# Graph network kernel: another order for the first loads, the ends of the layers, the branch and the tail

## The chip, the core and the metric

The kernel is one program on one core of a Trainium2 chip. The core has five engines with a queue of instructions each: PE (TensorE: matmuls; its weight loads are shown apart, as PEld), DVE (VectorE), ACT (ScalarE), POOL (GpSimd) and SP (SyncE, which only issues DMAs here). An engine takes its queue in order; semaphores make it wait for others. The metric is the device time of one execution in microseconds (us); smaller is better.

## The reference

Inputs are `x` (12,500 nodes x 256 features), 200,000 edges `src` -> `dst` sorted by `dst`, and weights. First come three layers that mix a node with the mean of its neighbours, then a norm, then one step of an attention over the same edges, and a second norm:

```python
def sage(x, Ws, Wn, b):
    agg  = segment_sum(x[src], dst)                # sum of the rows of the neighbours
    mean = agg / max(degree, 1)
    return x @ Ws + mean @ Wn + b

h = relu(sage(x, W0..)); h = relu(sage(h, W1..)); h = sage(h, W2..)
Z = layernorm(x + h)

ZU = einsum('nd,kdr->knr', Z, U)                   # 4 heads of 16
zs, zd = ZU[:, src], ZU[:, dst]
alpha = segment_softmax((zs * zd).sum(-1) / 4, dst)
agg = segment_sum(alpha * zs, dst)                 # per head
Zh  = .5 * Z + .5 * sum_k softmax(head_w)[k] * agg_k @ U_k.T
r   = Zh - (Zh @ Dmat.T) @ Dmat
out = layernorm(Z + relu(Zh + .5 * (r @ Dmat) - .05))
```

## The kernel before

**Groups of edges.** The sorted edges are cut into NG = 112 groups of GE = 1792: 128 partitions times GT = 14 columns (the last group has LT = 9 columns). For a group, `gather` (line 121) fetches the rows of its sources: 14 indirect DMAs on POOL, each for 128 edges, with the indices of one column of the list `srcI`. `onehot` (line 459, op in line 462) compares the edges' destinations with the 128 nodes that the group may hold; matmuls of that one-hot matrix with the gathered rows sum them by node into the PSUM tile `pA` (lines 866 and 874). A node whose edges straddle two groups is completed by `carry` (line 465), which adds the sum of the group before, shifted. `srcI` and `dstI` are lists that hold `src` and `dst` in this order of partition, group and column: pieces of 14 indices, 56 bytes, 128 x 111 of them in each.

**Preparation (lines 186 to 326).** The two lists are loaded on SP and ACT, then `dst` once more as `dall` in rows of 1600, from which DVE makes the start of each group (`rel`, `delta`, `starts`) and a flag that chooses between a fast and a general program. The weights of the attention are folded into two matrices `gz` and `gu` by PE and DVE. Meanwhile POOL gathers the rows of the first G0 = 3 groups into three buffers `xg` with a small list `src0` of their own. The same three buffers then rotate through all three layers.

**Layers (`fast_sage`).** Only a part of the nodes goes by gathers: 90 groups in layer 0, and 76 in layers 1 and 2. The last 20 or 32 blocks of 128 nodes are swept densely (`px`, line 755) with tables of edge counts, which are formed in layer 0 (`form`, with small gathers `el`). A group is a generator, `group(g)`, which yields at fixed points: gathers, one-hot and sums of the first half (7 columns); sums of the second half and carry; counts inverted, `mean` (line 908) and, in layer 0, a copy `agg` for the carry; transposes (`turned`, line 356); the four products with the two weight matrices (`sage_products`, line 349), `hn` and its store on SP as `hs_d`, which the next layer gathers from (`h_d`). The list `turns` in the loop says in which order the generators are advanced: `late` is group g-1, `now` is g, `far` is g-3 and exists only in layer 2, whose norm and projection follow. Between turns, units of the sweeps and the table work are put in. `chained` forces PE to take the groups' matmuls in the order of these turns. After the last group come one or two further rounds for the groups left over. In the last groups of layer 1, which the count table of layer 0 does not cover, 14 small matmuls (line 887) count the edges with `pT` as their target. Layer 2's last step writes `z_d`, its transpose `zt_d` and the projection `zu_d`.

**Branch and attention (`fast_attention`, line 969 on).** After layer 2 a maximum is compared with a bound (`calm`), and all engines branch on it. The attention has the same 112 groups with 14 gathers `zs` each (from `zu_d`), in six rotating buffers. A group has five steps: loads, gathers, one-hot and the logits (`pD`, line 1018, products in line 1026, exponents in line 1032); the sums `pA` (line 1042); the mean and its transpose (line 1056); the gradient step with `gz` and `gu` (lines 381 and 382); the norm and the store. A round of the loop begins a group and then advances each older one by a step, so group g is at its first step while g-4 is at its last; four further rounds empty the pipeline. `in_order` makes PE follow that order.

Four lines say how the turns were set:

```python
turns = [late, far, now, late, far, now, late]
if g > cut.NGS:
    turns = [far, far, live[-1], live[-1]]
for g in range(NG + 4):   # the attention: one new group, one step of each older one
```

## Time and profile before

| | |
|---|---|
| median of 3 runs | 8058.46 us (8031.01 to 8086.6) |
| the profiled execution, its own time | 6504.63 us |
| its span, first to last instruction | 6502.8 us |
| mean granted clock of TensorE in it | 0.815 |
| busy: PE | 5140.6 us (79%) |
| busy: DVE | 3906.3 us (60%) |
| busy: ACT | 3473.9 us (53%) |
| busy: POOL | 4809.5 us (74%) |

The profiled execution is 1554 us shorter than the median of the others. All times of single instructions, stages and waits come from it.

Where POOL is tells the stages apart, since each begins with its first gather and ends with its last:

| stage | POOL's gathers, us from the start |
|---|---|
| the three early groups | 4.2 to 61.7 |
| layer 0 | 68.9 to 1681.8 |
| layer 1 | 1705.5 to 3068.6 |
| layer 2 | 3099.1 to 4462.1 |
| attention | 4490.6 to 6466.7 |
| end of the span | 6502.8 |

The page shows the span in 40 slices of 162.6 us. A digit is the busy share of a slice in tenths, PEclk the granted clock of TensorE:

```profile
PE   4789999888799999998899999995555555555555
DVE  4867767555445555555456666665555655556555
ACT  2444555565466666664556666664454554545554
POOL 6767777777677777776777777776777777777775
PEclk8889999999899999998899999997555555555555
DMA  8978999898678888886788888885333333333332
```

The last 13 slices are the attention. The first slice and those in which a layer ends have lower digits than their neighbours.

### The profile page before, as it was taken

How to read it: one execution, taken by the hardware profiler on the slowest of the kernel's cores; microseconds unless marked ns; L12 is line 12 of the kernel's file. 1: busy time of each engine (PE TensorE's matmuls, PEld its weight loads, DVE VectorE, ACT ScalarE, POOL GpSimd, SP SyncE). 2: the span in 40 equal slices, each digit the busy share in tenths (PEclk: the TensorE clock that was granted, in tenths of full speed). 3: DMA queues.
4: the chain of work that ended last, by engine and by line, in shares of the span. 5: the costliest groups of instructions: out<-in, count | busy, mean ns of one | idle time of the engine just before them, and what ended most of it. 6: DMA issues, size and time to landing. Idle time of an engine off the chain costs nothing.

```text
span 8072.1 us, 86803 instructions
## 1 busy us (share of the span) xinstructions
PE 5552.0 (69%) x23570; PEld 4425.0 (55%) x23570; DVE 3882.7 (48%) x9939; ACT 3448.6 (43%) x6309; POOL 4798.8 (59%) x4977
## 2 busy tenths in 40 slices
PE   4677788767758888887678888888444444444445
PEld 3556566655546666666556766766333444444334
DVE  4655555433334444443444545554555555555555
ACT  2333333333335445554344444544344444444443
POOL 5655555555556656665466665656466666666665
PEclk7789888878879998999889999998655555555555
DMA  7766676666656666776566766776333333333332
GB/s 204 248 199 218 207 230 227 221 196 211 205 161 215 217 210 213 220 221 202 159 188 212 224 213 200 217 210 187 108 89 89 90 90 88 87 88 90 90 89 68
DMA packets 896774, 1391.65 MB, mean 172 GB/s; under 512 B 191216, under 2 KB 540424, under 8 KB 892173
## 3 DMA queue, kind: packets, MB, share of 16 engines
q1 hardware_dynamic: 650511, 834.50, 32.2%
q0 software_dynamic: 213152, 496.65, 21.9%
q10 hardware_dynamic: 32606, 54.81, 2.0%
q8 instruction: 189, 3.10, 0.2%
q14 instruction: 316, 2.59, 0.1%
HBM read 1175.15 MB, written 210.33 MB: 172 GB/s over the span
## 4 chain that ended last, share of the span: by engine, by line
PE 27%; DVE 9%; issue 6%; another core or an unknown queue 4%; DMA 3%; POOL 2%; ACT 1%; DVEq 0%; ACTq 0%; SPq 0%; POOLq 0%
PE px L755 7%; PE pD L1018 4%; PE pA L1042 4%; PE pA L866 3%; DMA zs<-zu_d,srcI 3%; PE pO L381 2%; PE pO L382 2%; DVE zz L1026 2%; POOL zs L121 2%; DVE lg L1029 2%; DVE wf L1035 1%; PE pO L354 1%; PE pA L469 1%; DVE hl L860 1%
## 5 line engine op out<-in xcount | busy, mean ns | idle before, releaser
L121 POOL DMA_INDIRECT xg<-h_d,srcI x2128 | 2077.6, 976 | 1413.2 <-issue 640.7
L755 PE MATMUL px<-c,hz 128*128 128x512 f32 x8232 | 2414.3, 434 | 313.7 <-issue 145.1
L755 PEld LDWEIGHTS px<-c,hz 128*128 128x128 f32 x8232 | 1611.9, 203 | 705.3 <-issue 212.1
L121 POOL DMA_INDIRECT zs<-zu_d,srcI x1563 | 1494.1, 956 | 830.5 <-issue 439.4
L749 ACT ACTIVATE c<-c 128x1024 fp32r<-128x1024 uint8 (+1 forms) x1274 | 1118.5, 890 | 1769.9 <-remote 629.5
L121 POOL DMA_INDIRECT xg<-in_x_dram,srcI x1218 | 1165.7, 957 | 968.6 <-PE pA L874 463.4
L462 DVE TENSOR_TENSOR oh<-rel,gconst 128x1792 fp32r<-128x1792 f32 (+1 forms) x354 | 714.0, 2017 | 1203.8 <-PE pO L382 597.5
L860 DVE TENSOR_TENSOR hl<-xg,hl 128x256 fp32r<-128x256 f32 x2128 | 777.3, 419 | 489.0 <-ACT hl L858 324.0
L1056 PE MATMUL pT<-ident,ag 128*64 128x128 f32 x112 | 47.2, 422 | 1167.2 <-DVE ag L392 400.3
L858 ACT ACTIVATE hl<-xg 128x512 fp32r<-128x512 f32 x1216 | 619.6, 567 | 258.8 <-PE pA L866 61.6
L1056 PEld LDWEIGHTS pT<-ident,ag 128*64 128x64 f32 x112 | 14.4, 129 | 1248.0 <-DVE ag L392 427.8
L866 PE MATMUL pA<-hl,oh 128*128 128x512 f32 x2128 | 607.0, 419 | 107.7 <-issue 78.8
L866 PEld LDWEIGHTS pA<-hl,oh 128*128 128x128 f32 x2128 | 417.7, 199 | 217.7 <-issue 94.4
L874 PE MATMUL pA<-xg,oh 128*128 128x258 f32 x1764 | 519.3, 457 | 4.0 <-DMA b<-in_L_gnn_b_dram 2.6
L874 PEld LDWEIGHTS pA<-xg,oh 128*128 128x128 f32 x1764 | 408.1, 237 | 95.1 <-issue 7.4
L645 ACT ACTIVATE win<-pc 128x392 uint16<-128x392 f32 x512 | 240.9, 494 | 445.6 <-PE pc L642 194.6
L1018 PE MATMUL pD<-z,ohT 128*128 128x128 f32 x1563 | 360.9, 418 | 53.2 <-DMA zb<-z_d 18.3
L344 DVE TENSOR_TENSOR pO<-b,pO 128x256 f32<-128x256 f32 x306 | 130.2, 426 | 554.7 <-remote 377.1
L633 DVE TENSOR_SCALAR oa<-iota,kt 128x128 bf16<-128x128 f16 x1024 | 264.8, 259 | 236.4 <-remote 88.8
L1018 PEld LDWEIGHTS pD<-z,ohT 128*128 128x128 f32 x1563 | 346.9, 333 | 54.0 <-issue 36.7
L368 DVE COPY hT<-pT 128x512 f32<-128x512 f32 x235 | 161.3, 687 | 443.5 <-remote 215.2
L642 PE MATMUL pc<-ob,oa 128*128 128x196 bf16 x1024 | 180.4, 265 | 274.7 <-ACT win L645 96.8
(257 smaller groups left out, 8265.2 us busy)
## 6 DMA issues: line engine op xcount, KB each, us to landing
hz<-hs_d SPq DMA_DIRECT2D x637, 512.0 KB
c<-cnt_d SPq DMA_DIRECT2D x112, 896.0 KB
ohT<-rel_d SPq DMA_DIRECT2D x111, 896.0 KB
hs_d<-hs SPq DMA_DIRECT2D x218, 256.0 KB
cnt_d<-win ACTq DMA_DIRECT2D x32, 1568.0 KB
xg<-h_d,srcI POOLq DMA_INDIRECT x2128
c<-cnt_d SPq DMA_DIRECT2D x70, 448.0 KB
zs<-zu_d,srcI POOLq DMA_INDIRECT x1563
```

Of the source, the lines that this page charges most:

```text
L121: return nc.gpsimd.indirect_dma_start(out=dst_ap, out_offset=None, in_=table, in_offset=bass.IndirectOffsetOnAxis(ap=idx, axis=0))
L462: nc.vector.tensor_tensor(oh[:, :m], r[:, :m].unsqueeze(2).to_broadcast([P, m, P]), nodes.unsqueeze(1).to_broadcast([P, m, P]), op=op)
L633: nc.vector.tensor_scalar(oa[:, c], iota16[:, :P], kt[:, 0, at], None, op0=OP.is_equal)
L645: nc.scalar.activation(win[:, :, d:d + 2 * NC].bitcast(U16).rearrange("p b (i t) -> p b i t", t=2), pc.rearrange("p i b t -> p b i t"), AF ...
L749: nc.scalar.activation(c32.rearrange("p (k d) -> p k d", d=P), c8[:, :, b % CB], AF.Copy)
L755: made.append(nc.tensor.matmul(px[f][i], hz[:, b % ZB, a:a + P].bitcast(F32R), c32[:, i * 512:(i + 1) * 512], start=b == 0 and part == 0, ...
L858: nc.scalar.activation(hi[:, b + j:b + j + n, :W], xg[:, a + j:a + j + n, :W], AF.Copy)
L860: nc.vector.tensor_tensor(lo[:, b + j, :D], xg[:, a + j, :D], hf[:, b + j, :D], op=OP.subtract)
L866: mm.append(nc.tensor.matmul(pa, oh[:, a + j], hl[:, j].rearrange("p i d -> p (i d)"), start=first, stop=stop))
L874: mm.append(nc.tensor.matmul(pa[:, :W], oh[:, a + j], xg[:, a + j, :W], start=first, stop=stop))
L1018: mm = [nc.tensor.matmul(pd[:, j * 2 * KR:(j + 1) * 2 * KR], ohT[:, a + j], z2.rearrange("p k i r -> p (k i r)"), start=True, stop=True) f ...
L1042: mm = [nc.tensor.matmul(pa, oh[:, j], w[:, j], start=j == 0, stop=g == 0 and j == T - 1) for j in range(T)]
```

## The change

It touches the order and the place of work; nothing is computed otherwise.

- **First loads.** `dall` is loaded first on SP, the weights of the attention (`dm`, `hw`, `uall`) first on ACT. `load_list` loads a part of a list. Half of `dstI` goes on each queue. `srcI` comes in five parts: the first on ACT behind the instruction `weighed`, the other four on SP, one ahead of each of the groups 1 to 4 of layer 0.
- **Ends of layers.** For the last group of a layer (`final`), `hb` alone is turned and multiplied with its weights ahead of the sums of the second half, and the mean alone is turned and multiplied behind them; in layer 0 its copy `agg` is left out. In layer 1's last groups the counting matmuls and the inversion of the counts stand ahead of the sums of their group, and are chained. From the last group on, `turns` has another order, with `near` = group g-2, and one further round in place of up to two. The compares of the first two groups of a layer are ordered behind the last result (`made`) of the layer before.
- **Branch.** The 28 gathers `zs` of the attention's first G1ST = 2 groups are issued in `fast_sage`, ahead of the branch, into one of the buffers `xg` (`ready`).
- **Tail of the attention.** When the last group begins, the remaining steps are advanced by a written order. The last group's product with `gz` is split off (`own_gradient`) and stands ahead of its sums.

In the diff, blank lines, hunks that only move a definition or name one result, and context are cut.

```diff
@@ -41,6 +41,7 @@
 G0 = 3
+G1ST = 2
 SMAX = 240.0
@@ -196,13 +205,27 @@
         nc.vector.memset(dall[:, EC:], PAD)
-        for t, ap, q in ((dstI, dst, nc.sync), (srcI, src, nc.scalar)):
-            q.dma_start(t[:, :NG - 1], ap[:last].rearrange("(g p j) -> p g j", p=P, j=GT))
-            q.dma_start(t[:full, NG - 1, :LT], ap[last:last + full * LT].rearrange("(p j) -> p j", j=LT))
-            if rest:
-                q.dma_start(t[full:full + 1, NG - 1, :rest], ap[E - rest:][None, :])
         nc.sync.dma_start(dall[:, :EC], dst.rearrange("(p j) -> p j", p=TE))
         nc.sync.dma_start(dall[:TE - 1, EC:], bass.AP(dst.tensor, EC, [[EC, TE - 1], [1, SL]]))
+        dm = load_w(prep, dmat, "dm")
+        hw = prep.tile([KR, K], F32, name="hw")
+        nc.scalar.dma_start(hw, head_w[None, :].to_broadcast([KR, K]))
+        uall = const.tile([P, DC, K, R], F32, name="uall")
+        for c in range(DC):
+            nc.scalar.dma_start(uall[:, c], u[:, c * P:(c + 1) * P, :].rearrange("k p r -> p k r"))
+        lists = [NG * i // 5 for i in range(6)]
+        def load_list(q, t, ap, a, b):
+            m = min(b, NG - 1)
+            i = q.dma_start(t[:, a:m], ap[a * GE:m * GE].rearrange("(g p j) -> p g j", p=P, j=GT))
+            if b == NG:
+                q.dma_start(t[:full, NG - 1, :LT], ap[last:last + full * LT].rearrange("(p j) -> p j", j=LT))
+                if rest:
+                    q.dma_start(t[full:full + 1, NG - 1, :rest], ap[E - rest:][None, :])
+            return i
+        load_list(nc.sync, dstI, dst, 0, NG // 2)
+        load_list(nc.scalar, dstI, dst, NG // 2, NG)
@@ -324,6 +341,7 @@
         nc.vector.tensor_scalar(gu, ptu[:KR, :], hrow, 0.5, op0=OP.mult, op1=OP.mult)
+        after(weighed, load_list(nc.scalar, srcI, src, 0, lists[1]))
@@ -375,12 +393,17 @@
-    def gradient_step(ps, zT, agT):
+    def own_gradient(ps, zT):
...
         mm = [nc.tensor.matmul(pg, zT[:, c], gz[:, c], start=c == 0, stop=False) for c in range(DC)]
-        mm.append(nc.tensor.matmul(pg, agT, gu, start=False, stop=True))
         return pg, mm[0], mm[-1]
+    def gradient_step(ps, zT, agT, own=None):
+        pg, first, _ = own_gradient(ps, zT) if own is None else (own, None, None)
+        last = nc.tensor.matmul(pg, agT, gu, start=False, stop=True)
+        return pg, first or last, last
@@ -456,17 +472,21 @@
-    def onehot(wk, nodes, r, dt=F32, name="oh", op=OP.is_equal, bufs=2, m=GT):
+    def onehot(wk, nodes, r, dt=F32, name="oh", op=OP.is_equal, bufs=2, m=GT, behind=None):
         oh = wk.tile([P, GT, P], dt, name=name, bufs=bufs)
-        nc.vector.tensor_tensor(oh[:, :m], r[:, :m].unsqueeze(2).to_broadcast([P, m, P]),
-                                nodes.unsqueeze(1).to_broadcast([P, m, P]), op=op)
+        i = nc.vector.tensor_tensor(oh[:, :m], r[:, :m].unsqueeze(2).to_broadcast([P, m, P]),
+                                    nodes.unsqueeze(1).to_broadcast([P, m, P]), op=op)
+        if behind is not None:
+            after(behind, i)
         return oh
...
         return nc.tensor.matmul(pa, sh, before, start=False, stop=True)
+    ready = []
@@ -828,7 +848,8 @@
                         halved = l or g > GB
-                        oh = onehot(wk, nodes, srel, F32R if halved else F32)
+                        oh = onehot(wk, nodes, srel, F32R if halved else F32, behind=closed[0] if g < 2 else None)
+                        final = g == cut.NGS - 1
                         ahead = l == 0 and g < G0
@@ -842,11 +863,34 @@
                                 hold_back(summed[-8 + 1 if j == 0 else -6], i)
+                        def invert(count):
+                            deg = wk.tile([P, 1], F32, name="deg")
+                            nc.vector.tensor_scalar_max(deg, count, 1.0)
+                            nc.vector.reciprocal(inv[:, g:g + 1], deg)
+                        if l == 1 and tail >= 0:
+                            pn = ps.tile([P, 2], F32, name="pT")
+                            mm = [nc.tensor.matmul(pn, oh[:, j], ones2, start=j == 0, stop=False) for j in range(GT)]
+                            mm.append(carry(wk, pn[:, 0:1], sdelta, edges_at[:, g - 1:g] if tail == 0 else lastn))
+                            chained(mm[0], mm[-1])
+                            invert(pn[:, 0:1])
+                            if not final:
+                                lastn = wk.tile([P, 1], F32, name="lastn")
+                                nc.vector.tensor_copy(lastn, pn[:, 0:1])
                         pa = ps.tile([P, 2 * D], F32, name="pA")
...
                         for a in (0, H):
+                            if a and final:
+                                hT, *mm = turned(wk, ps, [hb], "hTd")
+                                chained(*mm)
+                                po = ps.tile([P, D], F32, name="pO")
+                                mm = [nc.tensor.matmul(po, hT[:, c], wts[l][0][:, c], start=c == 0, stop=False)
+                                      for c in range(DC)]
+                                chained(mm[0], mm[-1])
                             if l:
@@ -879,25 +923,11 @@
                                 yield
-                        count = pa[:, D:D + 1]
-                        if l == 1 and tail >= 0:
-                            pn = ps.tile([P, 2], F32, name="pT")
-                            for j in range(GT):
-                                nc.tensor.matmul(pn, oh[:, j], ones2, start=j == 0, stop=False)
-                            held_ = edges_at[:, g - 1:g] if tail == 0 else lastn
-                            carry(wk, pn[:, 0:1], sdelta, held_)
-                            count = pn[:, 0:1]
                         yield
-                        if l == 0 or (l == 1 and tail >= 0):
-                            deg = wk.tile([P, 1], F32, name="deg")
-                            nc.vector.tensor_scalar_max(deg, count, 1.0)
-                            nc.vector.reciprocal(inv[:, g:g + 1], deg)
-                            if l and g + 1 < cut.NGS:
-                                lastn = wk.tile([P, 1], F32, name="lastn")
-                                nc.vector.tensor_copy(lastn, count)
-                        if l == 0 and g < cuts[ND].GS:
-                            nc.vector.tensor_copy(edges_at[:, g:g + 1], count)
+                        if l == 0:
+                            invert(pa[:, D:D + 1])
+                            if g < cuts[ND].GS:
+                                nc.vector.tensor_copy(edges_at[:, g:g + 1], pa[:, D:D + 1])
                         before = wk.tile([P, D + 2], F32, name="agg")
@@ -906,18 +936,28 @@
                         nc.scalar.activation(mean, sums, AF.Copy, scale=inv[:, g:g + 1])
-                        if not l:
+                        if not l and not final:
                             nc.scalar.activation(before[:, :W], pa[:, :W], AF.Copy)
...
                         light = l == L - 1 and g >= swept(l)
-                        hT, *mm = turned(wk, ps, [hb, mean], "hT", by_act=light)
+                        if final:
+                            hT, *mm = turned(wk, ps, [mean], "hTd")
+                        else:
+                            hT, *mm = turned(wk, ps, [hb, mean], "hT", by_act=light)
                         chained(*mm)
                         yield
-                        po, *mm = sage_products(ps, wts[l], hT)
-                        chained(*mm)
+                        if final:
+                            mm = [nc.tensor.matmul(po, hT[:, c], wts[l][1][:, c], start=False, stop=c == DC - 1)
+                                  for c in range(DC)]
+                            chained(mm[0], mm[-1])
+                        else:
+                            po, *mm = sage_products(ps, wts[l], hT)
+                            chained(*mm)
                         hn = lk.tile([P, D], F32, name="hn", bufs=4)
...
                         tiles, made = yield from finish(l, lk, ps, hn, po, light)
+                        if final:
+                            closed[0] = made
                         store_rows(tiles, at[0], made, at[1])
@@ -925,8 +965,10 @@
                     live, lag = [], 1 if l < L - 1 else 3
-                    for g in range(cut.NGS + min(lag, 2)):
+                    for g in range(cut.NGS + 1):
                         units = []
+                        if l == 0 and 0 < g < 5:
+                            load_list(nc.sync, srcI, src, *lists[g:g + 2])
                         if g < cut.NGS:
@@ -940,13 +982,16 @@
                         turns = [late, far, now, late, far, now, late]
-                        if g > cut.NGS:
-                            turns = [far, far, live[-1], live[-1]]
+                        if g >= cut.NGS - 1:
+                            near = live[g - 2] if far is not None else None
+                            turns = ([late, late, late, far, far, now, near, near, now] if now is not None else
+                                     [late, late, late] if near is None else [late, near, late, late, near, late, late])
+                            turns = [s for s in turns if s is not None]
                         n = len(turns)
...
                                 next(turns[i])
-                            if i == 2 and l == 0 and g < cut.NGS:
+                            if i == 2 and l == 0 and g < cut.NGS - 1:
@@ -958,6 +1003,12 @@
+            free = early[turn % G0][0].rearrange("p j d -> p (j d)")
+            for g in range(G1ST):
+                zs = free[:, g * GT * KR:(g + 1) * GT * KR].rearrange("p (j r) -> p j r", r=KR)
+                for j in range(GT):
+                    gather(zs[:, j], zu_d, srcI[:, g, j:j + 1])
+                ready.append(zs)
             t1 = wp.tile([P, 1], F32, name="t1")
@@ -993,8 +1044,8 @@
                                   .to_broadcast([P, T * P]))
-                zs = wk.tile([P, GT, KR], F32, name="zs", bufs=6)
-                for j in range(T):
+                zs = ready[g] if g < G1ST else wk.tile([P, GT, KR], F32, name="zs", bufs=6)
+                for j in range(T if g >= G1ST else 0):
                     i = gather(zs[:, j], zu_d, srcI[:, g, j:j + 1])
@@ -1038,6 +1089,10 @@
                 yield
+                own = None
+                if g == NG - 1:
+                    own, *mm = own_gradient(ps, zT)
+                    in_order(*mm)
                 pa = ps.tile([P, 2 * AW], F32, name="pA")
@@ -1057,7 +1112,7 @@
                 agT = attention_turned(wk, pt, P)
-                pg, *mm = gradient_step(ps, zT, agT)
+                pg, *mm = gradient_step(ps, zT, agT, own)
                 in_order(*mm)
@@ -1067,16 +1122,15 @@
             live = []
-            for g in range(NG + 4):
-                if g < NG:
-                    live.append(group(g))
-                    next(live[-1])
-                old = live[:-1] if g < NG else live
-                for s in old:
-                    next(s)
-                if g >= 4:
-                    live.pop(0)
-            assert not live
+            for g in range(NG):
+                live.append(group(g))
+                if g < NG - 1:
+                    order_of = [g, *range(max(0, g - 4), g)]
+                else:
+                    order_of = [g - 4] + [g - 3] * 2 + [g - 2] * 3 + [g] + [g - 1] * 4 + [g] * 4
+                for k in order_of:
+                    next(live[k])
+            assert all(next(s, 0) == 0 for s in live)
```

## The prediction, made before the changed kernel ran

> **What bounds the kernel now.** I read the groups of instructions first, then busy time by stage, then the waits of POOL, and last the timeline at the places where POOL stood still.
>
> ```profile
> L121 POOL DMA_INDIRECT xg<-h_d,srcI x2128 | 2076.2, 976 | 704.1 <-issue 288.6
> ...
> L121 POOL DMA_INDIRECT zs<-zu_d,srcI x1563 | 1499.1, 959 | 505.5 <-issue 425.4
> ...
> L121 POOL DMA_INDIRECT xg<-in_x_dram,srcI x1218 | 1172.4, 963 | 426.9 <-issue 136.9
> ```
> ```profile
> 3400.00:3700.00 300.00, 296.15 (x1406) 243.56 (x1405) 200.60 (x549) 183.87 (x315) 228.69 (x235) 1.00 0.87 269
> ...
> 4700.00:5000.00 300.00, 164.54 (x629) 138.20 (x629) 178.94 (x340) 152.26 (x255) 227.32 (x238) 0.50 0.37 103
> ```
>
> In the second block the columns are the window, then busy us and count of PE, PE weight loads, DVE, ACT and POOL, then granted clock, DMA share and GB/s. POOL's gathers take 0.95 us and are followed by 0.30 us in which it waits for nothing but its next issue: one per 1.254 us, 239 in 300 us. Both stages run at that rate (235 and 238), though PE is full in one and half idle in the other. All gathers (42 early ones, 1218, 2128, 1563 and 16 of `el`) make 4967 x 1.254 = 6230 us of a span of 6502.8. So POOL's queue is the kernel, and the rest is places where POOL stands still:
>
> ```profile
> POOL xg L121 <- PE pA L874: 130.7, 247, 10.8
> ...
> POOL xg L121 <- DMA hs_d<-hs: 54.2, 2, 30.5
> ...
> POOL zs L121 <- DVE gconst L456: 28.6, 1, 28.6
> ```
>
> That is the first layer, where POOL waits for a row buffer that PE has not summed yet; the two ends of layers (23.66 and 30.54 us); and the branch to the attention (28.56). After the last gather (6466.7) 36.1 us follow. In the order of instructions of the changed kernel all five engines stay in step except at these places and in the first tenth of the program, so no gather gets faster: only these stops can shrink.
>
> **Part 1, the first loads.**
>
> ```profile
> 1.27 21.05 SPq L201 DMA_DIRECT2D dstI<-in_dst_dram  x1
> ...
> 43.20 1.82 DVE L209 TENSOR_TENSOR viol<-dall 125x1600 f32<-125x1600 int32 x1 [11.66 <-DMA dall<-in_dst_dram]
> ...
> 60.74 0.98 POOL L121 DMA_INDIRECT xg<-in_x_dram,src  x1 [0.30 <-issue]
> ...
> 63.75 0.48 DVE L326 TENSOR_SCALAR gu<-pt,hrow 64x256 f32<-64x256 f32 x1 [0.21 <-PE pt L306]
> ...
> 68.86 0.97 POOL L121 DMA_INDIRECT xg<-in_x_dram,srcI  x1 [7.14 <-PE pA L874]
> ```
>
> Two lists of 128 x 111 pieces of 56 bytes (14,208 each) go out at once and hold SP for 21.05 and ACT for 24.41 us; `dall` stands behind them and is used from 43.20. All engines go on within 0.3 us of the end of `gu` (64.23). After: `dall` first, then only the dst list, half on each queue. Its price: both lists took 25.3 us, so half the pieces 12.7; `dall` before it 0.84 MB at the 172 GB/s of the first 100 us, 4.9; start at 2: it lands at about 20. DVE has by then done `viol` and `four`; left are three passes of `many`/`viol` and `vsum` (7.2), the chain from `brow` to `rel` (3.7, as at 27.8 to 31.5), and the rest as from 53.5 to 64.2 (10.7) with some 3 for PE round trips. Prep ends near 44 (38 if the list lands at 14, 52 if `dall` takes up to the 20 us it had), 20 us earlier.
>
> POOL's 42 early gathers still end at 61.7. The next one no longer waits for group 0: 7.14 - 0.30 = 6.8 saved. The next stops are 5.70 (at 91.8), 3.76 (112.8) and 10.01 (177.7), 18.6 above the issue gap. PE, ACT and DVE are 20 us ahead and POOL only 6.8, so 13 of it are in reach. Against this stand the src loads: four of the five parts, 11,368 pieces, now go through SP in groups 1 to 4, where windows of 20 us show DMA 0.97 to 1.02 busy. Trace: 25.3 us per 28,416 pieces, in an idle stretch. [...] I take 11, since prep also leaves the engines at 0.2 to 0.6 busy from 30 to 60 and the x loads start there. Bounds 3 and 18.6. The stops at 350.6, 487.1 and 1210.6 (10.0, 10.8, 7.1) stay: before the first of them DVE waits 13.13 us for `el`, whose gather lies at the same place of POOL's queue (10.5 groups) in both kernels. Part 1: **18** (10 to 25).
>
> **Part 2, ends of layers 0 and 1.**
>
> ```profile
> 3078.37 2.98 PE L887 MATMUL pT<-ones,oh 128*128 128x2 f32 x14
> ...
> 3084.20 2.05 PE L354 MATMUL pO<-ws,hT 128*128 128x256 f32 x4
> ...
> 3088.28 0.51 ACT L908 ACTIVATE mean<-agg,inv 128x256 f32<-128x256 f32 x1
> ...
> 3097.18 0.33 SPq L440 DMA_DIRECT2D hs_d<-hs  x1
> ...
> 3099.12 0.95 POOL L121 DMA_INDIRECT xg<-h_d,srcI  x1 [30.54 <-DMA hs_d<-hs]
> ```
>
> Layer 1: the counts' 14 matmuls (2.98) leave the middle of the sums. The carry ends at 3084.1 and `mean` starts at 3088.28, behind the group before's products, `hn` and `hs`; with those done earlier it needs `part`, `agg` and two handovers, 1.5 of 4.2: 2.7 saved. Own products ahead leave half of 3.8 behind the mean: 1.9, and the copy is 0.42 instead of 0.68: 0.3. The own turn and products (2.7) now lie before the second half, where the group before's transposes and copy lay: even. Sum 8 (5 to 11). Layer 0 has no count matmuls; its mean comes 2.8 after the carry, behind the next layer's compare (2.02): 1.8 saved, products 1.7, copy 0.3, less freed work in front 0.7: 4.5 (2 to 8). The delayed compares (2 x 2.0 us) run on DVE after the last `hs`; the first rows of layer 2 were used 8.1 us after POOL restarted, so they are covered; without cover they cost 4 per layer. The SP stores keep their order and places.
>
> **Part 3, the branch.** The last `zu` store is issued at 4484.78, `calm` is written at 4486.21, POOL starts at 4490.62. Now 28 gathers (35.1 us) stand before POOL's branch and wait only for the `zu` store: by the 1.9 us that the last `hs_d` store had from issue to POOL, 4486.7. The last group's own products ahead give about 1.5 more (1.03 of matmul, some copy). But POOL then pays its branch after them: between 0.3 (as DVE after `gu`) and 4.4 (calm to gather). I take 2.5: 3.9 + 1.5 - 2.5 = **3** (0 to 7). What is queued behind: group 2's gathers on POOL, and nobody waits for them for 35 us.
>
> **Part 4, the tail.**
>
> ```profile
> 6472.18 2.16 PE L1018 MATMUL pD<-z,ohT 128*128 128x128 f32 x9
> ...
> 6485.61 2.17 PE L1042 MATMUL pA<-w,oh 128*128 128x136 f32 x9
> ...
> 6491.72 2.07 PE L381 MATMUL pO<-gz,zT 128*128 128x256 f32 x4 [0.21 <-ACT g L406]
> ```
>
> From 6472.2 to 6495 PE does 22.8 us of work in order, at clock 0.50, with few gaps. The change puts gz/gu of two older groups (3.2 each) and a transpose ahead of the last group's pD: it moves from 6472.2 to about 6479. Then pA of the group before ends at 6484.4, its transpose and products at 6491, the own gz at 6493, pA at 6495, carry 6495.7, `ag` 6497.4, gu 6499: about **4 later** than now. For a gain: the own gz off the last chain (2.07) and exp no longer among the square roots (three table loads of 1.28). [...] The trace has 0.50 in every attention window, with bursts of 3.2 us and gaps, so I keep 0.50. -4 (-8 to +8).
>
> **Sum.** 18 + 4.5 + 8 + 3 - 4 = 29.5 us of the profiled execution's 6504.6 (span and 1.8 around it): 0.45%. The runs' median is 8058.5, 1.239 times that. No view shows why. [...] Then the stops, made of engine work, grow too: 29.5 x 1.24 = 37, 8022. Unscaled it would be 8029. I take **8021**.
>
> **The rivals.**
> 1. The lead of 20 us lasts: every stop behind pA in layer 0 (56 us above the issue gaps) goes and the tail gains 8, with layer ends at 12 and the branch at 7: 83 us, 1.3%, 7955. For it: PE is only 73 to 90% busy up to 500 us. Against: the stops at 350 and 487 follow `el`. Chance 0.22.
> 2. Slower: SP's queue. A list is 22 of 111 columns; by the 21.05 us a full one holds SP for 4.2, in front of x loads and hs stores on which ACT waits already (longest 6.3 and 7.7 us). If the busy DMA engines stretch a hold to 11, four cost 44 against 29.5: 14 slower, x 1.24, 8076. It decides from 7.4 us a list. For it: DMA at 0.97 to 1.02. Against: prep's lead. Chance 0.14.
> 3. It does not do what it says: the gathers ahead only move POOL's branch (0), the lead is used up at once (part 1 is 6.8), layer ends 10, tail -6: 11 us, 8045. Chance 0.14.
> The forecast has 0.5; its own range is 7990 to 8055 (15 to 45 us, and the runs' own spread of 28 to both sides in part).
>
> **How the numbers follow.** About 1%, 81 us, is what a measurement of this kernel tells from no change. Faster by that: rival 1 mostly and the forecast's end, 0.24. Slower by it: the far end of rival 2, where a busy queue holds SP for longer (24 us a list) than the idle one did for a whole list of both halves (21.05), 0.09. Within: 0.67. The range 7945 to 8080 takes rival 1's centre and rival 2's.
>
> **What would show it.** Right: POOL's wait at 69 gone and `gu` near 44; gaps between layers near 19 and 22.5; 28 gathers before the branch, then a gap under 4.4; pD of the last group after two older groups' products, and about 40 us after the last gather. Wrong: SP issues of srcI above 7 us; stops of POOL in the first 200 us as large as before; stops at 350 and 487 gone; a gap between layers above 28; a tail under 33.

## The result and the profile after

Fourteen runs of each kernel: the changed kernel 8076.34 us (8046.18 to 8123.26), the kernel before 8066.32 us (8012.91 to 8110.42), ratio 1.0016 (95% interval 0.9996 to 1.0037). The change brings nothing; the forecast of 0.45% less is outside the interval. On some chips both kernels take near 8060 us and on others near 6490; each ratio is taken on one chip, but by their times the page of before is from a chip of the second kind, and that of the changed kernel from one of the first. The same comparison on a chip of the second kind (e5 below) gave 1.0012 (1.0004 to 1.0021).

The groups of POOL on the page of the changed kernel (profiled run 8115.83 us, span 8114.0), then two of its 300 us windows, one in layer 2 and one in the attention (PE, PE weight loads, DVE, ACT, POOL busy and count, granted clock, DMA share, GB/s):

```profile
L122 POOL DMA_INDIRECT xg<-h_d,srcI x2128 | 2080.5, 978 | 1440.6 <-issue 648.0
L122 POOL DMA_INDIRECT zs<-zu_d,srcI x1535 | 1471.7, 959 | 769.0 <-issue 407.8
L122 POOL DMA_INDIRECT xg<-in_x_dram,srcI x1218 | 1170.3, 961 | 948.6 <-PE pA L918 437.7
```
```profile
4500.00:4800.00 300.00, 257.04 (x1153) 207.53 (x1152) 158.80 (x439) 144.28 (x249) 181.05 (x186) 0.94 0.70 217
7000.00:7300.00 300.00, 145.20 (x555) 121.95 (x555) 158.20 (x300) 134.51 (x225) 201.21 (x210) 0.50 0.30 91
```

A gather lasts as long as on the page of before (978 against 976 ns, 959 against 959), but POOL stands still for 1.5 to 2.2 times as long between them: 186 and 210 gathers in 300 us, where the prediction showed 235 and 238. The stops are not POOL's alone. On this page PE, too, stands still without a wait that the profile shows ("issue"), for 264.5 us in its three largest rows of this sort; among the 60 largest waits in the trace of before, down to 27.5 us, PE has none. The first two of the three (total, times, longest):

```profile
PE px L775 <- issue: 99.4, 87, 11.6
PE pA L910 <- issue: 85.6, 58, 17.1
```

So this page can't be laid beside that of before, line by line. The two kernels are compared on the pages of e1 and e5, both from chips of 6490 us. There, POOL's waits in the changed kernel:

```profile
POOL xg L122 <- issue: 474.8, 1454, 31.7
...
POOL xg L122 <- PE pA L918: 116.5, 253, 10.3
...
POOL xg L122 <- DMA hs_d<-hs: 44.7, 2, 25.3
...
POOL zs L122 <- PE pD L1069: 8.9, 2, 7.7
```

Against e1: the branch is now the 31.7 us in the first line (28.8 in e1), the waits for `pA` are 13 us less (129.4), those for the ends of layers 0 and 1 (`hs_d`) 3 us less (47.8), and the last line, 7.7 us for `pD` in the attention, is new.

### The profile page after: what moved, and what is told of

It is laid out like the page before. It is cut to its first block, busy times and chain, and to the rows that moved or that the text cites. A ratio compares the mean times of both kernels' runs of the same rounds, so it can differ in the third digit from the quotient of the medians.

```text
span 8097.0 us, 86815 instructions
## 1 busy us (share of the span) xinstructions
PE 5540.0 (68%) x23570; PEld 4413.5 (55%) x23570; DVE 3888.3 (48%) x9943; ACT 3447.8 (43%) x6307; POOL 4809.3 (59%) x4977
## 4 chain that ended last, share of the span: by engine, by line
PE 34%; DVE 9%; issue 8%; another core or an unknown queue 5%; DMA 4%; POOL 3%; ACT 2%; DVEq 0%; ACTq 0%; POOLq 0%
PE px L775 12%; PE pA L910 5%; PE pD L1069 4%; PE pA L1097 3%; DMA zs<-zu_d,srcI 3%; PE pO L399 2%; PE pO L372 2%; POOL zs L122 2%; PE pO L405 2%; DVE zz L1077 2%; DVE lg L1080 2%; DVE hl L904 1%; DVE wf L1086 1%; ACT hl L902 1%
## 5 line engine op out<-in xcount | busy, mean ns | idle before, releaser
L122 POOL DMA_INDIRECT zs<-zu_d,srcI x1535 | 1471.4, 959 | 774.4 <-issue 427.4
L478 DVE TENSOR_TENSOR oh<-rel,gconst 128x1792 fp32r<-128x1792 f32 (+1 forms) x354 | 713.7, 2017 | 1159.2 <-PE pO L405 528.4
L1097 PE MATMUL pA<-w,oh 128*128 128x136 f32 x1563 | 361.3, 418 | 0.0
```

Source lines behind the costliest of these rows:

```text
L122: return nc.gpsimd.indirect_dma_start(out=dst_ap, out_offset=None, in_=table, in_offset=bass.IndirectOffsetOnAxis(ap=idx, axis=0))
L478: i = nc.vector.tensor_tensor(oh[:, :m], r[:, :m].unsqueeze(2).to_broadcast([P, m, P]), nodes.unsqueeze(1).to_broadcast([P, m, P]), op=op)
L1097: mm = [nc.tensor.matmul(pa, oh[:, j], w[:, j], start=j == 0, stop=g == 0 and j == T - 1) for j in range(T)]
```

## The experiments

All times are medians beside the kernel before on the same chip, in five rounds unless said otherwise; the brackets are 95% intervals. Single gaps come from one trace of each kernel. e1 to e12 ran on chips of 6490 us, e13 to e18 on chips of 8060.

**The parts alone.** e1 is the kernel before, without an edit.

> The kernel before, unchanged: what two equal kernels differ by, and whether the profiled 6504.6 us is its usual time. Theory A (the runs are not in the condition of the page of before): its runs and its own profile lie near 8060 us, POOL stands still for over 1000 us in all where the page of before had some 73, and the gaps between stages are near 50 us as in the changed kernel. Theory B (only the parts of the change matter, the page of before is typical): its profile is near 6504 us, POOL's stops as before, gaps 23.7, 30.5 and 28.6 us. Ratio 1.000 by both.

6492.23 against 6493.43 us, ratio 0.9996 (0.9988 to 1.0005). The chip was one of 6490 us, so the page of before is typical of such a chip and of no other; neither theory had foreseen two kinds of chip. One number of that page is not typical: the gap between layers 1 and 2 was 30.5 us there and 25.4 here.

e2 has part 1 alone, e3 part 2 alone, e4 parts 3 and 4 alone: the hunks of the diff above, with nothing else. Their cores:

```diff
# e2
+        load_list(nc.sync, dstI, dst, 0, NG // 2)
+        load_list(nc.scalar, dstI, dst, NG // 2, NG)
+                        if l == 0 and 0 < g < 5:
+                            load_list(nc.sync, srcI, src, *lists[g:g + 2])
# e3
+                        if g >= cut.NGS - 1:
+                            turns = ([late, late, late, far, far, now, near, near, now] if now is not None else
# e4
+            for g in range(G1ST):
+                    order_of = [g - 4] + [g - 3] * 2 + [g - 2] * 3 + [g] + [g - 1] * 4 + [g] * 4
```

> The kernel before with part 1 of the change alone (first loads, lists in parts). Theory A: the lead is used up, 0.998 to 1.002. Theory B: the 18 us of the prediction times 1.24, 22 us less, 0.997. Theory C (the SP lists cost what is gained elsewhere): 14 us or more longer, 1.002 or above.

6482.1 us, 0.9982 (0.9974 to 0.9990): 11.3 us less.

> The kernel before with part 2 alone (ends of the three layers). Theory A: 0.998 to 1.002, with gaps between layers that are as long as in the kernel before when that runs as slowly. Theory B: 12.5 us and the 1.5 of layer 2, times 1.24, 17 us less, 0.998; the gaps are shorter by 4.5 and 8.

6498.27 us, 1.0009 (1.0001 to 1.0017): 4.8 us more.

> The kernel before with parts 3 and 4 alone (two attention groups gathered ahead of the branch, another order of the tail). Theory A: 0.998 to 1.002. Theory B, if parts 1 and 2 gain as forecast and the whole is 10 us longer: this one is some 49 us longer, 1.006, seen as a longer tail or a stop of POOL behind the branch.

6506.81 us, 1.0021 (1.0014 to 1.0028): 13.4 us more. Each part has an effect that stands clear of zero, so the parts do matter, as theory B has it; but all three of B's sizes missed (22 us less, 17 less, 49 more), and A's range of 0.998 to 1.002 holds e2 and e3. What speaks against A is e1, which ran in the condition of the page of before. The sum of the parts is 6.9 us more. e5, the changed kernel itself:

> The changed kernel itself beside the kernel before. Theory B (the whole is the sum of its parts as measured alone: first loads 11.3 us less, layer ends 5 more, branch and tail 13.4 more): 1.001, 7 us longer; POOL stops once for about 7.6 us at the 13th gather behind the 28 early ones, the last gather of layer 2 lies some 31 us ahead of the attention's first, and 40.9 us follow the last gather. Theory A (the lead of the first loads or the ends hides some of the costs): 0.999 or less, without that stop.

6499.51 against 6491.29 us, 8.2 us more: within the noise the whole is the sum of its parts.

**First loads.** POOL's timeline in e1 and e2 (start, duration, in brackets the idle time before it and what ended it): the first gather, and the stops of over 3 us up to 360 us.

```profile
4.32 1.10 POOL L121 DMA_INDIRECT xg<-in_x_dram,src  x1 [2.14 <-DMA src<-in_src_dram]
...
68.37 0.97 POOL L121 DMA_INDIRECT xg<-in_x_dram,srcI  x1 [6.69 <-PE pA L874]
...
91.58 0.95 POOL L121 DMA_INDIRECT xg<-in_x_dram,srcI  x1 [6.01 <-PE pA L874]
...
113.18 0.94 POOL L121 DMA_INDIRECT xg<-in_x_dram,srcI  x1 [4.41 <-PE pA L874]
...
178.23 0.94 POOL L121 DMA_INDIRECT xg<-in_x_dram,srcI  x1 [10.27 <-PE pA L874]
...
351.54 0.94 POOL L121 DMA_INDIRECT xg<-in_x_dram,srcI  x1 [10.15 <-PE pA L874]
```
```profile
10.25 1.10 POOL L121 DMA_INDIRECT xg<-in_x_dram,src  x1 [8.08 <-DMA src<-in_src_dram]
...
106.74 0.94 POOL L121 DMA_INDIRECT xg<-in_x_dram,srcI  x1 [3.42 <-PE pA L884]
...
165.02 0.94 POOL L121 DMA_INDIRECT xg<-in_x_dram,srcI  x1 [3.38 <-PE pA L884]
...
340.21 0.94 POOL L121 DMA_INDIRECT xg<-in_x_dram,srcI  x1 [9.88 <-PE pA L884]
```

Four stops of 27.4 us in all have become two of 6.8, and the stop near 350 keeps its length but comes 11.3 us earlier, as much as the whole gains. The one near 487, not shown, keeps its length too (10.4 and 10.1). The lists' price on SP is seen behind them: a list leaves SP in 0.4 us, but the load behind it on this queue is held, in e2 `hb` behind the first list and the last group's few pieces behind the fourth (the other `hb` loads of e2 take 0.4 to 1.4 us):

```profile
56.57 6.74 SPq L449 DMA_DIRECT2D hb<-in_x_dram  x1
149.91 5.32 SPq L222 DMA_DIRECT2D srcI<-in_src_dram  x1
```

And the first gather is 5.9 us late: it waits for its list `src0`, which no line of the change touches. e8 tests why:

```diff
+        tc.add_manual_dep(whole_dst.ins, first_list.ins.name, DONE, reason="the list of the first gathers lands alone")
```

> The changed kernel with the load of dall waiting until the small list of the first gathers has landed. Theory Q (the early gathers start 5.9 us later in the changed kernel since their list stands behind rows of dall in the DMA engines): first gather near 4.5 in place of 10.25, 6 us less than the changed kernel. Rival (the lead is used up by group 0's sums in any case): POOL stops some 6 us ahead of the first gather of layer 0, no difference.

First gather at 4.22; 6494.34 us, 1.0003 (0.9994 to 1.0011), 5.2 us less than e5, with intervals that overlap. So `src0` was held up by the rows of `dall` moved ahead of the other loads: shown for the first gather, not for the time. Part of the lead is used up at once: POOL's three stops between 80 and 170 us make 13.2 us in e8 (two of 6.8 in e2), and layer 0's last gather ends only 0.2 us earlier than in e5. The same edit once more is e12.

**The branch.** SP's and PE's timelines behind the branch, in e1:

```profile
4487.50 0.36 SPq L435 DMA_DIRECT2D zn<-zu_d  x1
4488.27 0.34 SPq L435 DMA_DIRECT2D zb<-z_d  x1
...
4498.38 3.25 PE L1018 MATMUL pD<-z,ohT 128*128 128x128 f32 x14 [17.65 <-DMA zb<-z_d]
```

in e5, with POOL's first gather ahead of the branch and its stop:

```profile
4472.79 0.37 SPq L455 DMA_DIRECT2D zn<-zu_d  x1
4502.19 0.35 SPq L455 DMA_DIRECT2D zb<-z_d  x1
...
4512.07 3.25 PE L1069 MATMUL pD<-z,ohT 128*128 128x128 f32 x14 [46.88 <-DMA zb<-z_d]
```
```profile
4467.14 0.94 POOL L122 DMA_INDIRECT xg<-zu_d,srcI  x1 [31.74 <-issue]
...
4524.46 0.94 POOL L122 DMA_INDIRECT zs<-zu_d,srcI  x1 [7.69 <-PE pD L1069]
```

In e1 SP issues `zb` 0.77 us after `zn`. In e5 it takes 29.4. SP's waits from 4465 to 4515 us show why:

```profile
SPq L455 <- DMA xg<-zu_d,srcI: 28.7, 3, 25.0
```

These are waits for landings of the early gathers, three in a row, by semaphores that stand in the program ahead of `zb`; the last ends at 4502.0, when one of the last gathers has landed (the 28th is issued at 4500.85). Why the program ties this load to them, though it reads none of their data, the record does not show. `zT` and `ohT` stand behind `zb`, PE's first `pD` comes 44.9 us after POOL's first gather instead of 12.9, and POOL, which runs on, reaches a gather that is held to `pD` and stops. e6 halves the early gathers:

```diff
-G1ST = 2
+G1ST = 1
```

> The changed kernel with 14 gathers ahead of the branch in place of 28. Theory SP (SP's first loads behind the branch wait until the early gathers have landed, and all of the attention's first work waits for these loads): SP issues zb 17.5 us earlier, the stop of 7.6 us is gone, 7 us less than the changed kernel. Rival (the stop is a start-up of the attention that comes anyway when POOL runs ahead): a stop of the same length, moved by less than a group; no difference. Rival (POOL's own branch now shows): a gap of 0.3 to 4.4 us behind the 14.

6491.02 us, 1.0002 (0.9993 to 1.0010), 8.5 us less than e5. In its trace:

```profile
4485.54 0.37 SPq L455 DMA_DIRECT2D zn<-zu_d  x1
4498.62 0.35 SPq L455 DMA_DIRECT2D zb<-z_d  x1
...
4508.59 3.25 PE L1069 MATMUL pD<-z,ohT 128*128 128x128 f32 x14 [30.55 <-DMA zb<-z_d]
```

POOL begins at 4479.74; `zb` follows after 18.9 us (35.1 in e5), `pD` after 28.9 (44.9), and no stop of POOL over 1.4 us is left in the attention. Theory SP holds. POOL's own branch, behind the gathers, showed no gap above 0.31 us in either.

**The ends of layers.** PE's rows at the end of layer 2 (`xg<-h_d` ends at 4456.62 in e1, 4451.18 in e3), with the mean and the write of `calm`. e1, then e3:

```profile
4463.27 1.89 PE L866 MATMUL pA<-hl,oh 128*128 128x512 f32 x7
...
4465.80 1.88 PE L866 MATMUL pA<-hl,oh 128*128 128x512 f32 x7
4467.52 0.59 PE L469 MATMUL pA<-agg,sh 128*128 128x256 f32 x2
...
4481.08 0.14 DVE L967 TENSOR_SCALAR calm<-t 1x1 int32<-1x1 f32 x1
```
```profile
4461.39 1.88 PE L894 MATMUL pA<-hl,oh 128*128 128x512 f32 x7
...
4466.14 1.98 PE L894 MATMUL pA<-hl,oh 128*128 128x512 f32 x7
4467.96 0.59 PE L471 MATMUL pA<-agg,sh 128*128 128x256 f32 x2
...
4481.00 0.14 DVE L994 TENSOR_SCALAR calm<-t 1x1 int32<-1x1 f32 x1
```

In e1 the first half's sums begin 6.7 us after the last gather, the carry ends after 11.5, `calm` after 24.6. In e3 it is 10.2, 17.4 and 30.0: the chain behind the carry is 0.5 us shorter, and the carry 5.9 later. From such rows, in us: last gather to the end of the carry / carry to the last `hs` (in layer 2: `calm`) / whole gap of POOL. e7 and e9 also have gathers ahead of the branch, which shortens their third gap (by 3.0 us in e4 against e1).

| | layer 0 | layer 1 | layer 2 |
|---|---|---|---|
| e1, before | 10.0 / 8.2 / 22.4 | 13.4 / 9.0 / 25.4 | 11.5 / 13.1 / 28.8 |
| e3, part 2 | 11.0 / 4.8 / 20.0 | 16.0 / 6.1 / 25.1 | 17.4 / 12.6 / 34.4 |
| e7, first half first | 15.2 / 5.6 / 25.2 | 16.4 / 6.1 / 25.8 | 16.4 / 11.7 / 29.6 |
| e9, tile freed | 11.0 / 6.9 / 22.6 | 15.8 / 6.8 / 27.1 | 13.0 / 17.8 / 32.5 |

Behind the carry the change brings 3.4 and 2.9 us in layers 0 and 1. In front of it, it takes 1.0, 2.6 and 5.9. A single gap is uncertain: e5 and e8, equal at these ends, have 19.5 and 22.5 for layer 0, 25.3 and 30.0 for layer 1. What holds in all traces is seen by laying the five with the old ends (the page of before, e1, e2, e4, e10) beside the four with the new (e3, e5, e6, e8). From the last gather to the end of the carry:

| | layer 0 | layer 1 | layer 2 |
|---|---|---|---|
| old ends | 9.8 to 10.4 | 12.5 to 15.5 | 10.4 to 11.5 |
| new ends | 9.3 to 13.2 | 15.8 to 21.8 | 17.3 to 18.1 |

So the loss in front of the carry is clear in layer 2, smaller and less certain in layer 1, and not shown in layer 0. e7 lets the first half go ahead of the products of the group before:

```diff
-turns = ([late, late, late, far, far, now, near, near, now] if now is not None else
+turns = ([late, far, now, late, far, late, near, near, now] if now is not None else
```

> The changed kernel with the last group's sums of the first half ahead of the products of the group before (turns late, far, now, late, far, late, near, near, now in the last group's round). Theory W (the change holds these sums back behind the chain of mean, transpose and products of the group before, 2.6 us at the end of layer 1 and 5.9 at the end of layer 2): the sums end 2 to 6 us earlier after the last gather, 6 to 10 us less than the changed kernel. Rival (the end is set by the handovers behind the last sum): gaps as in the changed kernel, no difference.

6498.12 us, 1.0011 (1.0003 to 1.0019), 1.4 less than e5: no difference clear of the noise. The first sums begin at 3.1 and 5.7 us after the last gather in layers 1 and 2 (10.2 in e3), but the carry ends at 16.4 as before: the wait has moved between the halves. Theory W falls as it was put: not the first half's place, but all of the chain of the group before stands ahead of the second half. e9 takes it out of there, at the price of one DVE addition that the end then doesn't need:

```diff
-                        if g >= cut.NGS - 1:
+                        if g == cut.NGS:
...
+                                nc.vector.tensor_add(base, wts[l][2], po)
...
+                            po = ps.tile([P, D], F32, name="pO")
...
+                        sage_end(lk, l, (None, None, base) if final else wts[l], po, hn, xb)
```

> The changed kernel with the turns of the kernel before in the last group's round; the last group's own products still stand between its two halves, but leave their PSUM tile at once (their sum with the bias goes to SBUF), so that the products of the group before can come after the second half. Theory P (what holds the last sums back is that the whole chain of the group before must run ahead of the own products, since both need the one tile pO): the carry ends 10 to 11 us after the last gather in layer 0, 14 to 15 in layer 1, 12 to 13 in layer 2 (16 and 17.4 in the changed kernel's last two), the chains behind it stay at 5, 6 and 12.5; about 6 us less than the changed kernel, 1.000 to 1.001. Rival (PE has so much work there that order does not matter): the carries end as late as in the changed kernel, no difference.

6500.24 us, 1.0010 (1.0002 to 1.0018): no gain. The carry in layers 0 and 2 is at 11.0 and 13.0 us, near where theory P has it, and in layer 1 at 15.8, later than it has it; but the chain behind the carry of layer 2 is 17.8 in place of 12.6, as the norms of two older groups now stand there. What is taken out in front of the sums comes back behind them.

**Together.** e10 has part 1 and 14 gathers ahead; e11 also the ends of e9; e12 also the list of e8. The tail is that of the kernel before in all three. Of e11's edit, against the changed kernel:

```diff
-G1ST = 2
+G1ST = 1
-                if g == NG - 1:
+                if False:
-            for g in range(NG):
+            for g in range(NG + 4):
```

> The kernel before with part 1 and with 14 gathers ahead of the branch; ends of layers and tail as before. If the parts add up: 11.3 us less for the first loads and 3 less at the branch, 14 us less, 0.998.

6481.43 us, 0.9981 (0.9974 to 0.9988): 12.8 us less.

> As the one before, and with the ends of layers of e9 as well (tail as in the kernel before). If the parts add up: another 4 us less where theory P holds, 18 us less than the kernel before, 0.997; if the ends bring nothing, as the one before.

6489.44 us, 0.9993 (0.9984 to 1.0001): 8.0 more than e10, which neither half of the expectation had. In the traces the gap of layer 2 is 33.1 us against 25.2, those of layers 0 and 1 differ by less than 1: with these ends the loss is layer 2's.

> As e11, with the load of dall behind the landing of the first gathers' list. If layer 0 ends when the other engines' lead lets it and not when POOL starts: no difference to e11, although the first gathers start 6 us earlier. Rival: 5 us less.

6480.55 us, 0.9979 (0.9972 to 0.9986): 8.9 less than e11. The expectation of no difference fell, but the list's worth stays open: layer 0's last gather ends 4.2 us earlier than in e11, and the rest of the 7.7 us between the two traces lies in layer 2's end and the attention, which the list doesn't touch.

**On the other kind of chip.** e13 is the changed kernel with the end of layer 2 as before; e14 has the first loads with the list alone, 14 gathers ahead, new ends in layers 0 and 1 alone, and the tail as before.

```diff
-                        final = g == cut.NGS - 1
+                        final = g == cut.NGS - 1 and l < L - 1
```

> The changed kernel with the end of layer 2 as in the kernel before. If that end carries the loss: the gap ahead of the attention is near 26 us in place of 31.7, 5.5 us less than the changed kernel, 1.0003. If the ends of layers 0 and 1 lose too, or the loss lies elsewhere: no difference to the changed kernel, 1.001.

> First loads with the list of the first gathers alone, 14 gathers ahead of the branch, new ends in layers 0 and 1 alone, tail as in the kernel before. If the parts add up: 12.8 us less as in e10, another 5 to 9 for the list, 2 to 3 for the end of layer 0: 20 to 25 us less than the kernel before, 0.9965. If layers 0 and 1 bring nothing: 18 to 22 less, 0.997.

The chip was one of 8060 us: 0.9995 (0.9970 to 1.0020) and 0.9982 (0.9961 to 1.0004). Both kernels again, e15 and e16, on another such chip: 1.0004 (0.9976 to 1.0033) and 1.0000 (0.9975 to 1.0024). The kernel of e14 a third time, e18: 0.9982 (0.9960 to 1.0005). Nothing is decided by e13 and e15; e14, e16 and e18 allow a gain of 0.1% there and don't show one. The 20 to 25 us expected of this kernel on a chip of 6490 us were not tried: no such chip ran it.

e17, in three rounds, is the kernel before without the last of the 14 gathers of each group in layers 1 and 2; the sums then use rows of an earlier group in that column.

```diff
-                        for j in range(0 if ahead else GT):
+                        for j in range(0 if ahead else GT - (l > 0)):
```

> The kernel before with 13 of the 14 gathers of each group in layers 1 and 2 (the last column's rows are left as an earlier group had them): 152 gathers less, 152 x 1.254 = 191 us of POOL's time. On a chip of 6490 us, if POOL's queue is the bound of these layers: 150 to 191 us less, 0.971 to 0.977. On a chip of 8060 us, if POOL is the bound there too: 191 us less, 0.976. If PE's signals to the other engines set the pace there: under 40 us less, above 0.995, with longer stops of POOL.

7709.02 against 7970.28 us, 0.9671 (0.9634 to 0.9709): 261 us less, 1.72 for each gather left out, more than the 1.254 that a gather has on POOL's rows, and more than the 191 that were expected. A window of its layer 2:

```profile
4300.00:4600.00 300.00, 273.14 (x1244) 219.29 (x1243) 171.35 (x471) 159.79 (x276) 182.14 (x187) 0.97 0.74 225
```

POOL issues 187 gathers in 300 us, 186 with 14 of them in a group (the window shown of the changed kernel, from another chip of this kind), while PE, DVE and ACT all do more in the same time. Whole layers on e17's own chip say the same: from first to last gather, layers 1 and 2 take 1.54 and 1.62 us a gather in e17 and 1.56 and 1.63 in e18, though PE, DVE and ACT have as much work in a group of 13 gathers as in one of 14. So the gathers set the pace on this chip too; the theory that PE's signals do falls. Why one takes 1.6 us there, though its own rows are 0.95 and 0.30 as elsewhere and the rest is stops about once in a group, was not found.

## Why the prediction was wrong

The sum was 29.5 us less; on a chip of 6490 us, where its durations come from, it is 8.2 more (e5). By its steps:

- **Bound.** POOL's queue as the bound holds for chips of 6490 us and, by e17, in substance for those of 8060, where a gather costs more (1.72 us in place of 1.254). The factor 1.24 was drawn from one page and the runs of another chip; that the stops grow by it, from 29.5 to 37 us, was the author's estimate, and no run shows it. What the runs show in its place: POOL's gather and its issue gap are 0.95 and 0.30 us on both kinds of chip, and POOL's idle time ahead of its gathers is 1.5 to 2.2 times as long on the page of the changed kernel as on that of before.
- **Part 1** (18; measured 11.3). The mechanism is right; prep ends at 48.9 (44 forecast). The term "6.8 saved" in front of layer 0 is the one that was mis-sized. It came to nothing: the 42 early gathers end at 68.3 and not "still at 61.7", since the list they need is held up. The stops after it gave 11.3 by 350 us, where 11 were taken. The bound of 3 takes 10.1 us for the lists in groups 1 to 4 off the 13 (25.3 us x 11,368 of 28,416 pieces, an estimate from the row); no run shows that term, and e2 gains 11.3 with its lists. What did cost is a small list behind the rows of `dall`, in a place that the prediction never looked at: the first gather at 10.25 us in e2, 4.32 in e1 and 4.22 in e8. Rival 2's cost is there, but small: held loads and lists make some 14 us over the four lists, less than half of its 7.4 a list, and part 1 still gains. The 21.05 us from which it was sized are such a held load too: line 201 loads the last group behind the whole list, which had itself left SP in 0.46. That its 8076 is the measured median is luck.
- **Part 2** (12.5 less; measured 4.8 more) is the step that failed. "The own turn and products now lie before the second half, where the group before's transposes and copy lay: even" counted instructions and left out the handovers to other engines. With `late` three times ahead of `now`, PE, whose order is fixed by hand, must run through mean, transpose, copy and products of the group before, with the waits between them, ahead of the last sums. Behind the carry 3.4 and 2.9 us come in (3.8 and 4.9 by the prediction's terms); in front of it, where 0.7 and 3.0 were to be gained in layers 0 and 1, the same traces lose 1.0 and 2.6, and 5.9 in layer 2. The 5.9 were costed at nothing: the only mention of that end was a gain of 1.5 in part 3. That the handovers are the cause is argued from the rows and from e7 and e9, where the loss moved and did not go; no run removed it and kept the gain.
- **Part 3** (3 less). The gap shrank by 3.0 in e4, and POOL's branch cost nothing, where 2.5 was taken. That 3.0 is the forecast's sum is luck: e4 has the old end of layer 2 and so none of the 1.5 in it, and the first term came to 3.0 in place of 3.9. The failed words are "nobody waits for them for 35 us": SP did, for the loads that all of the attention's first work needs. The stop of 7.6 us was not in any rival. Gap, stop and tail together make 9.3 of e4's 13.4; the rest was not located.
- **Part 4** (4 more; 4.75 in e4) was sized right by its own working: `pD` of the last group comes 13.4 us after the last gather in place of 5.6. The granted clock stayed at 0.50 in e5's last 42 us, in which PE is busy for 27.43, so the 0.50 of the prediction holds. No run shows the gain of 8 us that its range and rival 1 have for the tail: 40.9 us follow the last gather in e5, 36.1 on the page of before.

The last rows of e5 in the attention, PE, for part 4 (the last gather ends at 6447.92):

```profile
6461.29 2.18 PE L1069 MATMUL pD<-z,ohT 128*128 128x128 f32 x9
...
6473.15 2.07 PE L399 MATMUL pO<-gz,zT 128*128 128x256 f32 x4 [0.56 <-ACT g L429]
6474.66 2.38 PE L1097 MATMUL pA<-w,oh 128*128 128x136 f32 x9
```

The third line, the last group's sums, is what the end waits for. It begins 26.7 us after the last gather, 19.0 in e1: the work of older groups and the own `gz` (second line) that were put ahead of it delay it by 7.7 us, and what is left behind it is 3.0 us shorter.

Rival 1 fell with the stops at 350 and 487, which stayed; PE's "73 to 90% busy up to 500 us" holds from 200 us on only (it was 39% up to 100 us, 66% from there to 200). The third rival, that the change doesn't do what it says, comes nearest in its sum: 11 us less. With the stop behind the branch (7.6) and layer 2's longer gap (5.6 in e3), which no rival had, that would be 2 us more, against the 8.2 measured.

## What to carry to other kernels

When work is moved ahead of another piece in a hand-made order, count the handovers between engines that the moved piece contains, not its instructions: in e3 the chain of the group before stood ahead of the last sums, and at the end of layer 2 the carry came 5.9 us later. When transfers are put ahead of a branch, ask which queue on the far side waits for all that is still under way, and how long that queue's first transfer is waited for: SP's took 29.4 us in e5, 0.77 in e1. A page from one chip need not describe the chips on which the time is measured (6504.63 us here, against a median of 8058.46): one run of the unchanged kernel beside it shows whether it does.

## What was not expected of the hardware

Two kinds of chip run the same program in 6490 and in 8060 us. Two pages of the changed kernel show it, one from a chip of the slow kind (a second one, span 8097.0 us) and that of e5 (6488.8). Instructions of DVE, ACT and POOL last about as long on both (`oh` 2017 and 2018 ns, `c` 890 and 892, a gather `zs` 959 and 958), PE's matmuls in part longer on the slow kind (`pA<-xg` 452 against 397 ns, `px` 433 against 414, `pD` 418 on both). Of the 1608 us between the two spans, PE's busy time makes 394, that of the three others differs by less than 26: the rest is stops, on all engines. No chip was measured at two times, so whether this is the chip or its state at that hour is not shown. On a chip of 8060 us a gather left out saved 1.72 us. And a list of small pieces left SP in 0.4 us, while the next load on that queue was held for up to 6.7 (e2). SP's wait of 29.4 us behind the branch, on the other hand, is the program's own, by its semaphores.
